# Layer 0's head norms on ScalarE with accumulated sums, two heads at a time, and layer 0's value scaling on VectorE

## The chip, the cores and the metric

The kernel runs on one core of one Trainium2 chip. The metric is the device time of one execution in microseconds; three executions of the kernel before gave 3661.22, 3663.64 and 3666.74 us, median 3663.64 us. The profile was taken of one more execution, with a span of 3660.5 us and a mean granted TensorE clock of 0.985.

## The reference

Two graph attention layers, one after the other, on 16 graphs of 1024 nodes with 256 features. Layer 0 (4 heads of 64 features), cut to what the change touches:

```
h = einsum('bnd,hde->bhne', x, W)                     # values per head
weight = leaky_relu(e_src[i] + e_dst[j]) masked by adj == 0
dst = softmax(weight) @ h + bias
out = relu(dst) + h
mu, var = out.mean(-1), out.var(-1)                   # over the 64 features of one head
out = (out - mu) / sqrt(var + 1e-6) * ln_gamma + ln_beta
x = layernorm(x + out)                                # over all 256 features
```

Layer 1 normalises its input, runs masked attention of 8 heads of 32 features in which queries, keys and values are the same tensor, adds the result, and applies an MLP of width 1024 with an exact Gelu; a last layer norm ends it.

## The kernel before

Everything in fp32 apart from the adjacency, which becomes a uint8 mask. A graph's 1024 nodes are 8 blocks of 128 rows, and 2 halves (n) of 512 rows.

Four engines execute an order fixed at build time (`manual_schedule`, L760). Two generators, `layer0()` and `layer1()`, yield after each step an estimated cost; the loop at L762 takes the next step from layer 0 of graph b+1 or from layer 1 of graph b. Which one is decided by `wanted()` and the table `COURSE` (L747): it says how far layer 0 should be when layer 1 is at a given place. So layer 0 of the next graph always runs beside layer 1 of this one, and in the steady state one graph after another repeats the same pattern. Post-processing is written as chains: `begin(chain, wait)` puts a generator on a list, and `advance` runs its next part when the planned clock has moved on by what the chain yielded. `complete(chain)` runs a chain's remaining parts at once. These yields decide only where instructions are recorded[...].

Layer 0 of a graph:

- `prepare` (L286): per pair of row blocks it transposes x (L227, copied by ScalarE at L230), turns the adjacency into a mask (transposes at L295, a squaring ScalarE activation with an accumulated sum at L296), and multiplies x by the weights W with the attention columns beside them (L322) into a PSUM tile `ph` named "acc". ScalarE then takes from `ph` the source terms (L323), `v0`'s last column exp(e) (L324), `dinv` (L325), and four times, once per head, the 64 value columns times that exp (L327): these products are the operand `v0` of the attention. VectorE adds the bias to the same `ph` for the residual `hb` (`take_h`, L347), at a planned distance of 1.5. "acc" has 2 buffers.
- `attention0` (L350): 16 steps. VectorE builds the weights `p` of a step (four instructions at L374, tile `p0`), TensorE multiplies them with `v0` (64 matmuls, L389). After each head of a half `relu_residual` (L418 to L430) divides, applies the relu and adds to `hb`.
- `after0` (L432): when the fourth head of a half is done, it normalises all 4 heads and 4 row blocks (128 x 1024 elements) together: sum (L445), centring (L446), square on ScalarE (L451), sum of squares (L454), variance (L455), `power` on GpSimd (L198) for the inverse root, gamma (L457), beta added to x (L458), scaling (L460), addition (L461). Then the layer norm over 256 features (L465 to L479) and layer 1's inputs: `normed` (L214 through `scale_shift`), x1 (L484), nT by transposes (L227, L233), v1 (L494).

Layer 1 of a graph: `attention1` (L502), 32 steps: TensorE makes four score tiles of 128x512 (L517) in the four PSUM buffers `ps`, ScalarE exponentiates them (L522), VectorE masks them one step later (L528), TensorE multiplies with the values two steps later (L535, L542). `mlp` (L629): first product (L637, also in `ps`), Gelu on ScalarE (L644), second product (L650), `last_norm` (L678).

`half(n)` (L724) hands layer 1 the results of `after0`; step jb = 4 of `attention1` is the first that needs half 1.

Of the kernel before, what the change touches and what calls it, by code (L numbers as in the profile page):

```python
# [31 lines left out]
F32 = mybir.dt.float32  # L32
# [3 lines left out]
AF = mybir.ActivationFunctionType  # L36
OP = mybir.AluOpType
PSUM = bass.MemoryType.PSUM

P = 128  # L40
# [10 lines left out]
def fast_path(  # L51
# [192 lines left out]
    def begin(chain, wait):  # L244
        chains.append([clock[0] + wait, chain])
# [40 lines left out]
    def prepare(b, hb, esr, v0, dinv, mask):  # L286

        def turn_mask(k):  # L290
            i = b * NB + k
            ak = adj_blocks.pop(i)
            pt = ps_a.tile([P, NB, P], BF16, name="acc")
            for j in range(NB):
                nc.tensor.transpose(pt[:, j, :], ak[:, j * P : (j + 1) * P], identb)  # L295
            nc.scalar.activation(  # L296
                mask[k // BPH][:, :, k % BPH * P : (k % BPH + 1) * P],
                pt,
                AF.Square,
                bias=shift_c,  # L300
                scale=-(NEAR0 + NEAR1),
                accum_out=types[:, i : i + 1],
            )
            load_adj(i + 3)

        for k in range(0, NB, GB):
            i = b * (NB // GB) + k // GB
            load_blocks(i + 1)
            xk = x_blocks.pop(i)
            xT = one.tile([P, DC, GB * P], F32, name="xT")  # L310
            transpose_rows(xT, xk)
            yield 0.45
            turn_mask(k)
            yield 0.5
            if k % BPH == 0:

                finish_norms(b - 1, k // BPH)
                hb.append(one.tile([P, BPH, D], F32, name=f"hb{k // BPH}"))
            for g in range(GB):
                ph = ps_a.tile([P, D + 2 * H0], F32, name="acc")  # L320
                for c in range(DC):
                    nc.tensor.matmul(ph, xT[:, c, g * P : (g + 1) * P], w0e[:, c, :], start=c == 0, stop=c == DC - 1)  # L322
                nc.scalar.copy(apart[g][:, :, 0], ph[:, D + H0 : D + 2 * H0])  # L323
                nc.scalar.activation(v0[:, k + g, :, HO], ph[:, D : D + H0], AF.Exp)  # L324
                nc.scalar.activation(dinv[:, k + g, :], ph[:, D : D + H0], AF.Exp, scale=-0.99)  # L325
                for hd in range(H0):
                    nc.scalar.mul(  # L327
                        v0[:, k + g, hd, 0:HO], ph[:, hd * HO : (hd + 1) * HO], v0[:, k + g, hd, HO : HO + 1]
                    )
                begin(take_h(hb[-1][:, (k + g) % BPH, :], ph), 1.5)  # L330
                yield 0.9
                if g == 0:
                    turn_mask(k + 1)
                    yield 0.5
            turning = turn_sources(esr[:, k * P : (k + GB) * P])
            begin(turning, 0.4)
        complete(turning)
# [5 lines left out]
        nc.scalar.copy(dst, es.rearrange("p g q -> p (g q)"))  # L343
        yield from ()

    def take_h(h, ph):
        nc.vector.tensor_add(h, ph[:, 0:D], bias0_r)  # L347
        yield from ()

    def attention0(b, hb, v0, esr, dinv, factors, mask, rinv):  # L350
# [81 lines left out]
    def after0(b, n, hd, av, o, rinv):  # L432


        relu_residual(av, hd, o, rinv)
        if hd < H0 - 1:
            return
        yield 1.5
        heads = [P, BPH * H0, HO]
        rowwise = [P, BPH, D]  # L440
        xl = one.tile(rowwise, F32, name="xl")
        load_x(xl, b, n * BPH, BPH)
        oh = o.rearrange("p g (h e) -> p (g h) e", e=HO)
        s = small.tile([P, BPH * H0], F32, name="s0")
# [6 lines left out]
        nc.scalar.activation(sq, o, AF.Square)  # L451
        yield 2.5
        v = small.tile([P, BPH * H0], F32, name="v0s")
        nc.vector.tensor_reduce(v, sq.rearrange("p g (h e) -> p (g h) e", e=HO), axis=mybir.AxisListType.X, op=OP.add)  # L454
        nc.vector.tensor_scalar(v, v, 1.0 / HO, EPS_HEAD, op0=OP.mult, op1=OP.add)  # L455
        r = power(v, BPH * H0, "r0")
        nc.vector.tensor_mul(o, o, lng0_r[:, None, :].to_broadcast(rowwise))  # L457
        nc.vector.tensor_add(xl, xl, lnb0_r[:, None, :].to_broadcast(rowwise))  # L458
        yield 3.0
        nc.vector.tensor_mul(oh, oh, r[:, :, None].to_broadcast(heads))  # L460
# [38 lines left out]
        handed[b, n] = x1, v1, nT  # L499
# [718 lines left out]
```

## Time and profile before

| engine | busy us | share of the span | instructions |
|---|---|---|---|
| PE (TensorE matmul) | 3452.5 | 94% | 64417 |
| PEld (weight load) | 2304.6 | 63% | 64417 |
| DVE (VectorE) | 2986.7 | 82% | 5328 |
| ACT (ScalarE) | 2156.0 | 59% | 4732 |
| POOL (GpSimd) | 384.5 | 11% | 360 |

Busy time is time in which an instruction of the engine was under way; a matmul that waits inside the pipeline still counts, so 94% is an upper bound of what TensorE did. DMA moved 33 GB/s on average and is not near a limit. Groups that the change touches, by line:

| line, engine | count | mean ns | busy us |
|---|---|---|---|
| L327 ACT, values times exp, 128x64 from PSUM | 512 | 315 | 118.6 |
| L451 ACT, square, 128x1024 | 32 | 1054 | 33.7 |
| L347 DVE, residual, 128x256 | 128 | 422 | 54.0 |
| L445, L454 DVE, sums | 32 each | 1215, 1214 | 38.9, 38.9 |
| L446, L457, L460 DVE, 128x1024 | 32 each | 1225, 1217, 1220 | 39.2, 39.0, 39.1 |
| L455 DVE, 128x16 | 32 | 174 | 5.6 |
| L198 POOL, 128x16 | 32 | 3815 | 122.1 |

Where the mean times the count exceeds the busy time, as at L327, neighbouring instructions overlapped: 118.6 us over 512 is 232 ns of engine time for each.

### The profile page before, as it was taken

How to read it: one execution, taken by the hardware profiler on the slowest of the kernel's cores; microseconds unless marked ns; L12 is line 12 of the kernel's file. 1: busy time of each engine (PE TensorE's matmuls, PEld its weight loads, DVE VectorE, ACT ScalarE, POOL GpSimd, SP SyncE). 2: the span in 40 equal slices, each digit the busy share in tenths (PEclk: the TensorE clock that was granted, in tenths of full speed). 3: DMA queues.
4: the chain of work that ended last, by engine and by line, in shares of the span. 5: the costliest groups of instructions: out<-in, count | busy, mean ns of one | idle time of the engine just before them, and what ended most of it. 6: DMA issues, size and time to landing. Idle time of an engine off the chain costs nothing.

```text
span 3660.5 us, 142025 instructions
## 1 busy us (share of the span) xinstructions
PE 3452.5 (94%) x64417; PEld 2304.6 (63%) x64417; DVE 2986.7 (82%) x5328; ACT 2156.0 (59%) x4732; POOL 384.5 (11%) x360
## 2 busy tenths in 40 slices
PE   5699999999999999999999999999999999999998
PEld 4458476575766757566585765757667575665846
DVE  4888788887878888788887988888788887888884
ACT  2474846647466574755747566474665747557464
POOL 0101101010110101101011010101101011010110
PEclk9799999999999999999999999999999999999999
DMA  4110201102010110201102011020101102010000
GB/s 106 28 23 16 46 6 42 18 26 36 13 41 12 33 29 14 45 7 38 23 16 46 6 40 20 26 36 13 41 12 32 31 14 45 7 38 9 16 6 14
DMA packets 77669, 97.67 MB, mean 27 GB/s; under 512 B 9088, under 2 KB 60160, under 8 KB 77056
## 3 DMA queue, kind: packets, MB, share of 16 engines
q0 software_dynamic: 18432, 33.56, 6.4%
q1 hardware_dynamic: 52736, 50.35, 4.4%
q8 instruction: 506, 8.29, 0.9%
q10 hardware_dynamic: 5888, 4.60, 0.4%
q14 instruction: 107, 0.88, 0.1%
HBM read 105.26 MB, written 16.78 MB: 33 GB/s over the span
## 4 chain that ended last, share of the span: by engine, by line
PE 63%; DVE 26%; issue 4%; ACT 3%; POOL 3%; DMA 1%; ACTq 0%; SPq 0%; DVEq 0%; POOLq 0%
PE ps L517 13%; PE po L535 10%; PE ps L637 9%; PE acc L389 9%; DVE p L528 7%; PE po L650 7%; PE po L542 6%; DVE p L374 6%; PE acc L322 3%; POOL r L198 3%; DVE st L203 2%; PE acc L295 1%; PE acc L227 1%; PE ps L363 1%; DVE mv L204 1%
## 5 line engine op out<-in xcount | busy, mean ns | idle before, releaser
L528 DVE TENSOR_TENSOR p<-p,mask 128x1024 f32<-128x1024 f32 x1024 | 1199.1, 1218 | 160.7 <-ACT p L522 156.9
L522 ACT ACTIVATE p<-ps 128x512 f32<-128x512 f32 x2048 | 1059.6, 614 | 329.6 <-PE ps L517 327.8
L517 PE MATMUL ps<-nT 32*128 32x512 f32 x4096 | 769.1, 654 | 12.6 <-ACT cb L365 10.0
L374 DVE SCALAR_TENSOR_TENSOR p<-cb,dinv,mask 128x512 f32<-128x512 f32 x1024 | 698.4, 744 | 0.5 <-ACT cb L365 0.5
L542 PEld LDWEIGHTS po<-v,p 128*32 128x32 f32 x32768 | 390.0, 110 | 334.2 <-issue 239.5
L389 PE MATMUL acc<-v,p 128*64 128x65 f32 x16384 | 556.4, 225 | 43.8 <-DVE p L374 42.7
L389 PEld LDWEIGHTS acc<-v,p 128*64 128x64 f32 x16384 | 511.5, 139 | 118.0 <-DVE p L374 65.2
L644 ACT ACTIVATE hid<-ps,b_sb 128x256 f32<-128x256 f32 x512 | 235.5, 471 | 555.4 <-PE ps L637 555.1
L535 PE MATMUL po<-p,v 128*32 128x512 f32 x2048 | 550.2, 612 | 10.4 <-DVE p L528 8.9
L535 PE MATMUL po<-p,unit 128*32 128x512 f32 x2048 | 549.5, 612 | 0.0
L637 PE MATMUL ps<-yT,w_sb 128*128 128x256 f32 x2048 | 491.6, 387 | 0.7 <-issue 0.7
L650 PE MATMUL po<-w_sb,hid 128*128 128x256 f32 x2048 | 465.0, 381 | 0.0
L650 PEld LDWEIGHTS po<-w_sb,hid 128*128 128x128 f32 x2048 | 385.4, 190 | 64.0 <-issue 11.4
L637 PEld LDWEIGHTS ps<-yT,w_sb 128*128 128x128 f32 x2048 | 376.2, 191 | 64.3 <-issue 12.2
L542 PE MATMUL po<-v,p 128*32 128x33 f32 x32768 | 387.6, 198 | 7.5 <-DVE o L584 3.1
L517 PEld LDWEIGHTS ps<-nT 32*128 32x128 f32 x4096 | 268.0, 186 | 170.8 <-issue 56.8
L535 PEld LDWEIGHTS po<-p,v 128*32 128x32 f32 x2048 | 78.7, 109 | 387.5 <-DVE p L528 204.5
L198 POOL TENSOR_TENSOR r<-v,mhalf 128x1 f32<-128x1 f32 (+1 forms) x160 | 158.1, 988 | 1009.2 <-DVE v L684 721.7
L296 ACT ACTIVATE mask<-acc,shift_c 128x1024 uint8<-128x1024 bf16 x128 | 144.3, 1127 | 44.3 <-PE acc L295 43.8
L322 PE MATMUL acc<-w0e,xT 128*128 128x264 f32 x512 | 146.2, 409 | 20.9 <-DVE hb L347 20.8
L278 POOL DMA_DIRECT2D ak<-in_adj_dram x128 | 69.7, 545 | 878.1 <-PE acc L295 864.7
L198 POOL TENSOR_TENSOR r<-v1s,mhalf 128x4 f32<-128x4 f32 x32 | 34.9, 1092 | 1132.2 <-DVE ranges L418 891.0
(116 smaller groups left out, 2929.2 us busy)
## 6 DMA issues: line engine op xcount, KB each, us to landing
ak<-in_adj_dram POOLq DMA_DIRECT2D x128, 256.0 KB, 3.9
xk<-in_x_dram SPq DMA_DIRECT2D x64, 256.0 KB, 2.8
xl<-in_x_dram SPq DMA_DIRECT2D x32, 512.0 KB, 4.0
out_dram<-z SPq DMA_DIRECT2D x128, 128.0 KB, 1.7
w_sb<-in_L_gnn_W_dram ACTq DMA_DIRECT2D x2, 1024.0 KB, 10.2
v<-in_L_gnn_a_src_dram ACTq DMA_DIRECT2D x1, 640.0 KB, 7.8
v<-in_L_gnn_a_dst_dram ACTq DMA_DIRECT2D x1, 640.0 KB, 3.8
w0e<-in_L_gnn_W_dram ACTq DMA_DIRECT2D x8, 32.0 KB, 7.3
```

The lines of the kernel that those rows point to most:

```text
L198: nc.gpsimd.tensor_tensor(r, src, mhalf[:, :n], op=OP.pow)
L322: nc.tensor.matmul(ph, xT[:, c, g * P : (g + 1) * P], w0e[:, c, :], start=c == 0, stop=c == DC - 1)
L374: nc.vector.scalar_tensor_tensor(p[:, i, :], cb[:, hd % PAIR, :], dinv[:, j2 + i, hd : hd + 1], mask[n][:, j2 + i, :], op0=OP.max, op1=OP. ...
L389: nc.tensor.matmul(av[at : at + TILE, q, :], ps[i // 2][:, i % 2, q * P + at : q * P + at + TILE], v0[:, j4 + i, hd, :], start=j4 + i == 0 ...
L517: nc.tensor.matmul(tiles[e], of_keys[q, quad, keys], of_queries[q, quad, :], start=True, stop=True)
L522: nc.scalar.activation(p[:, i, :], tiles[e + i], AF.Exp, scale=SCALE1)
L528: nc.vector.tensor_mul(p, p, mask[n][:, jb, None, :].to_broadcast([P, PAIR, HALF]))
L535: nc.tensor.matmul(moved[at * Q : (at + 1) * Q, :], v, ps[0][:, e, :], start=jb == 0, stop=jb == NB - 1)
L542: nc.tensor.matmul(held[at : at + Q, q, e, :], ps[1][:, e, q * P + at : q * P + at + Q], values[:, hd, :], start=jb == 0 and e == 0 and q ...
L637: nc.tensor.matmul(ph, w1_sb[:, c, f * P : (f + 1) * P], yT[:, c, q * P : (q + GB) * P], start=c == 0, stop=c == DC - 1,)
L644: nc.scalar.activation(hid[f // 4][:, f % 4, :], ph, AF.Gelu, bias=b1_sb[:, f : f + 1], scale=1.0)
L650: nc.tensor.matmul(po, hid[f // 4][:, f % 4, g * P : (g + 1) * P], w2_sb[:, f, :], start=f == 0, stop=f == FC - 1,)
```

## The change

The four scaling activations per row block in `prepare` leave ScalarE. VectorE does them as one product of 128x256 inside `take_h`, after the bias addition, with exp broadcast over the 64 columns of a head.

The norm per head runs for two heads of a half at a time, so a first chain starts when the second head is done and a second one after the fourth. VectorE sums (128x512 to 128x8) and scales by -1/64 to get minus the mean. ScalarE squares each 128x64 piece with minus the mean as its bias and accumulates the sum itself (8 activations per pair of heads, all into the same scratch tile `sq0`); centring and the second sum on VectorE go. After `power`, VectorE multiplies minus the mean by the inverse root, and ScalarE applies scale and shift with 8 Identity activations of 128x64, in place of VectorE's product. Gamma follows, on the two heads. Beta and x are added once for the half. The purpose is to even out the load of the two engines over the stages. The table `COURSE` is set to 1.42 and 15.0 where it had 1.45 and 14.0: layer 0 gets a little less of its work placed beside `attention1` and a little more beside `mlp`, and ends one planned unit earlier.

```diff
@@ prepare
-                for hd in range(H0):
-                    nc.scalar.mul(
-                        v0[:, k + g, hd, 0:HO], ph[:, hd * HO : (hd + 1) * HO], v0[:, k + g, hd, HO : HO + 1]
-                    )
-                begin(take_h(hb[-1][:, (k + g) % BPH, :], ph), 1.5)
+                begin(take_h(hb[-1][:, (k + g) % BPH, :], v0[:, k + g, :, :], ph), 1.5)
...
-    def take_h(h, ph):
+    def take_h(h, v, ph):
         nc.vector.tensor_add(h, ph[:, 0:D], bias0_r)
+        nc.vector.tensor_mul(
+            v[:, :, 0:HO],
+            ph[:, 0:D].rearrange("p (h e) -> p h e", e=HO),
+            v[:, :, HO : HO + 1].to_broadcast([P, H0, HO]),
+        )
@@ after0
         relu_residual(av, hd, o, rinv)
+        if hd % PAIR < PAIR - 1:
+            return
+        yield 1.0
+        heads = slice((hd - PAIR + 1) * HO, (hd + 1) * HO)
...
+        nc.vector.tensor_reduce(mean, oh, axis=mybir.AxisListType.X, op=OP.add)
+        nc.vector.tensor_scalar(mean, mean, -1.0 / HO, None, op0=OP.mult)
+        yield 1.5
...
+        for g, e in rows_of:
+            nc.scalar.activation(
+                sq, oh[:, g, e, :], AF.Square, bias=mean[:, g, e : e + 1], accum_out=v[:, g, e : e + 1]
+            )
+        yield 2.2
+        nc.vector.tensor_scalar(v, v, 1.0 / HO, EPS_HEAD, op0=OP.mult, op1=OP.add)
+        r = power(v.rearrange("p g e -> p (g e)"), BPH * PAIR, "r0").rearrange("p (g e) -> p g e", e=PAIR)
...
+        yield 2.5
+        nc.vector.tensor_mul(mean, mean, r)
+        if hd == H0 - 1:
+            nc.vector.tensor_add(xl, xl, lnb0_r[:, None, :].to_broadcast(rowwise))
+        yield 0.4
+        for g, e in rows_of:
+            nc.scalar.activation(
+                oh[:, g, e, :], oh[:, g, e, :], AF.Identity, bias=mean[:, g, e : e + 1], scale=r[:, g, e : e + 1]
+            )
+        yield 2.2
+        pair = o[:, :, heads]
+        nc.vector.tensor_mul(pair, pair, lng0_r[:, None, heads].to_broadcast([P, BPH, PAIR * HO]))
         if hd < H0 - 1:
             return
...
-        nc.vector.tensor_reduce(s, oh, axis=mybir.AxisListType.X, op=OP.add)
-        nc.vector.scalar_tensor_tensor(
-            oh, s[:, :, None].to_broadcast(heads), -1.0 / HO, oh, op0=OP.mult, op1=OP.add
-        )
-        yield 2.0
-        sq = one.tile(rowwise, F32, name="sq")
-        nc.scalar.activation(sq, o, AF.Square)
-        yield 2.5
...
-        nc.vector.tensor_reduce(v, sq.rearrange("p g (h e) -> p (g h) e", e=HO), axis=mybir.AxisListType.X, op=OP.add)
...
-        nc.vector.tensor_mul(oh, oh, r[:, :, None].to_broadcast(heads))
+        for first in range(PAIR - 1, H0 - 1, PAIR):
+            complete(norms[b, n, first])
         nc.vector.tensor_add(o, o, xl)
-        yield 2.0
+        yield 0.5
...
-    COURSE = [(0.0, 1.0), (ATTN1, 1.45), (WORK1 - 14.0, 2.0), (WORK1, 2.0)]
+    COURSE = [(0.0, 1.0), (ATTN1, 1.42), (WORK1 - 15.0, 2.0), (WORK1, 2.0)]
```

More of the change, by code (lines that the diff above doesn't have):

```diff
@@ L435, in after0 @@
         relu_residual(av, hd, o, rinv)
+        if hd % PAIR < PAIR - 1:
+            return
+        yield 1.0
+        heads = slice((hd - PAIR + 1) * HO, (hd + 1) * HO)
+        oh = o[:, :, heads].rearrange("p g (h e) -> p g h e", e=HO)
+        rows_of = [(g, e) for g in range(BPH) for e in range(PAIR)]
+        mean = small.tile([P, BPH, PAIR], F32, name="s0")
+        nc.vector.tensor_reduce(mean, oh, axis=mybir.AxisListType.X, op=OP.add)
+        nc.vector.tensor_scalar(mean, mean, -1.0 / HO, None, op0=OP.mult)
@@ new lines, in after0 @@
+        yield 1.5
+        v = small.tile([P, BPH, PAIR], F32, name="v0s")
+        sq = one.tile([P, HO], F32, name="sq0")
+        for g, e in rows_of:
[5 more added lines that the diff above has]
+        r = power(v.rearrange("p g e -> p (g e)"), BPH * PAIR, "r0").rearrange("p (g e) -> p g e", e=PAIR)
@@ new lines, in after0 @@
+        rowwise = [P, BPH, D]
+        if hd == H0 - 1:
+            xl = one.tile(rowwise, F32, name="xl")
+            load_x(xl, b, n * BPH, BPH)
+        yield 2.5
+        nc.vector.tensor_mul(mean, mean, r)
+        if hd == H0 - 1:
+            nc.vector.tensor_add(xl, xl, lnb0_r[:, None, :].to_broadcast(rowwise))
[4 more added lines that the diff above has]
+            )
@@ L436, in after0 @@
+        yield 2.2
+        pair = o[:, :, heads]
+        nc.vector.tensor_mul(pair, pair, lng0_r[:, None, heads].to_broadcast([P, BPH, PAIR * HO]))
         if hd < H0 - 1:
             return
[L438 to L444, printed above, removed]
-        nc.vector.tensor_reduce(s, oh, axis=mybir.AxisListType.X, op=OP.add)
@@ L446, in after0 @@
-        nc.vector.scalar_tensor_tensor(
-            oh, s[:, :, None].to_broadcast(heads), -1.0 / HO, oh, op0=OP.mult, op1=OP.add
-        )
-        yield 2.0
-        sq = one.tile(rowwise, F32, name="sq")
-        nc.scalar.activation(sq, o, AF.Square)
-        yield 2.5
-        v = small.tile([P, BPH * H0], F32, name="v0s")
-        nc.vector.tensor_reduce(v, sq.rearrange("p g (h e) -> p (g h) e", e=HO), axis=mybir.AxisListType.X, op=OP.add)
-        nc.vector.tensor_scalar(v, v, 1.0 / HO, EPS_HEAD, op0=OP.mult, op1=OP.add)
@@ L456, in after0 @@
[L456 to L460, printed above, removed]
+        for first in range(PAIR - 1, H0 - 1, PAIR):
+            complete(norms[b, n, first])
         nc.vector.tensor_add(o, o, xl)
-        yield 2.0
+        yield 0.5
         mv = small.tile([P, BPH, 2], F32, name="mv0")
```

## The prediction

> **What bounds the kernel.** I read the chain of waits first, then busy time by stage, then the timeline of one graph.
>
> ```profile
> PE 63%; DVE 26%; issue 4%; ACT 3%; POOL 3%; DMA 1%; ACTq 0%; SPq 0%; DVEq 0%; POOLq 0%
> ```
>
> TensorE carries most of the chain, VectorE a quarter; ScalarE's 3% says nothing yet, since a matmul that waits for a PSUM buffer counts as PE. So I cut one graph (222 us) into stages.
>
> ```profile
> 1492.36:1560.00 67.64, 63.31 (x1458) 33.73 (x1444) 49.26 (x69) 55.47 (x138) 3.96 (x9) 0.97 0.25 44
> 1560.00:1611.50 51.50, 50.13 (x1325) 27.34 (x1327) 50.14 (x64) 32.52 (x70) 1.46 (x2) 1.00 0.05 9
> 1611.50:1702.65 91.15, 89.10 (x1117) 75.92 (x1117) 74.96 (x174) 36.39 (x65) 15.11 (x11) 1.00 0.06 16
> 1702.65:1724.00 21.35, 18.62 (x288) 8.68 (x288) 20.85 (x44) 17.60 (x40) 4.12 (x4) 0.92 0.25 63
> ```
>
> Columns after the length: PE, PEld, DVE, ACT, POOL. Layer 1's attention beside `prepare` (first row) has ScalarE at 82%, VectorE at 73%. Its end, beside the first steps of `attention0`, has VectorE at 97%. The MLP (third row) has PE at 98%, ScalarE at 40%. The passage to the next graph has VectorE at 98%, ScalarE at 82%.
>
> PE's busy time hides its waits, so I compared runs of equal matmuls in the timeline: eight score matmuls (L517) follow one another in 1.07 us if nothing holds them.
>
> ```profile
> 1514.53 1.14 PE L517 MATMUL ps<-nT 32*128 32x512 f32 x8
> 1514.92 0.93 ACT L327 ACTIVATE v<-acc,v 128x64 f32<-128x64 f32 x4
> 1515.71 2.07 ACT L522 ACTIVATE p<-ps 128x512 f32<-128x512 f32 x4
> 1517.16 1.80 PE L517 MATMUL ps<-nT 32*128 32x512 f32 x8
> ```
>
> The four exponentials start only after L327's 0.93 us, the `ps` buffers come free late, and the next score run takes 0.66 us more. I summed such excess over the shortest of its kind for one graph (1702.65 to about 1925): some 23.6 us of 222. Of it 7.1 lie in the passage, 5.5 in the `prepare` stretch (3.65 in score runs like the one shown), 6.8 in the rest of `attention1`, 4.2 in the MLP. About 198 us per graph is TensorE's own work, which the change leaves alone. It can only move these 23.6.
>
> The passage hangs on the second half's norm:
>
> ```profile
> 1696.22 1.05 ACT sq L451
> 1697.30 1.23 DVE v0s L454
> ...
> 1698.81 3.83 POOL r L198
> 1702.65 1.24 DVE hb L460
> ...
> 1712.14 2.27 DVE p L528 x2
> ...
> 1716.86 2.08 ACT sq L214 x4
> ```
>
> Square, sum, power, scaling, then statistics between mask products (L528), then the activation whose result TensorE transposes for layer 1's fifth step: it waits 2.4 us there.
>
> [...]
>
> **The change, part by part.**
>
> *ScalarE, prepare.* L327 goes: 118.6 us, 0.93 us per row block, 7.4 per graph. Everything else on its queue there moves up by as much. In the 19 us of a pair of blocks TensorE's own work is about 17 us, and ScalarE then has about 15, so most score stalls of this stretch (0.66 to 0.81 each, below 0.93) should vanish: -3.5 us per graph, and -0.5 where mask transposes wait for the copy of x. The last two row blocks lie in the next stretch: -1.2.
>
> *VectorE, prepare.* 128 products of 128x256 from PSUM; L584 has the same form at 424 ns: +54.3 us, 3.4 per graph. This stretch has 18 us of VectorE idle, and the residual before it waited 73.1 us in all for L327, which ends. `ph` is held 0.42 us longer, but its buffer is wanted again some 4 us later: nothing.
>
> *VectorE, norms.* L446, L454, L460 go: -117.2 us. [...] Small ones at 0.16 to 0.17 (L455, L475): 64 times minus-mean and mean-times-root, and 32 more variances: +26. Net -81, or 5 us per graph, nearly all in the MLP and the passage. With the products VectorE falls by about 26, to 2961 us. In the MLP TensorE runs almost gapless, so this gives nothing directly there.
>
> *ScalarE, norms.* The trace has no 128x64 square with accumulation. [...] Its accumulator read is 209 ns at L296, where it overlaps the activation's end by 100. In the built order squares 2 to 8 of a burst each wait for the one before (same scratch tile). [...] I take 0.45, so 3.6 us per burst (2.7 to 4.3). [...] ScalarE rises by about 250, to 2404 us. The squares all fall into the MLP, which has 55 us of ScalarE idle per graph against 14.4 for them. Behind a burst wait Gelus (which free the `ps` buffers for L637) and exponentials for `cb`; on VectorE the variance waits for the burst, and `p` for TensorE queues behind it. Four buffers and the 2.02 us runs of L389 cover most: I charge +0.5 us per graph.
>
> *GpSimd.* Two 128x8 powers of 2.07 us replace one 128x16 of 3.8; the one on the passage's path is 1.7 us shorter.
>
> *The passage.* In the built order the last Identity burst stands behind the four exponentials of the next graph's first step, and gamma and the addition stand behind the mask products of the first two. From the first score run on (before: activation for TensorE at +14.2): exponentials end at +3.1, Identity +5.8, copy of x and second exponentials +8.4, masks +9.6, [...] statistics and variances +14.1, masks of the third step +16.4, residual and value product +17.3, then the activation at about +17.4. Before, scaling and addition were done ahead of those masks. So +3.2 us per graph on the path that ends the wait; the shorter power lies before it and is lost.
>
> *COURSE.* One `attention0` step (3 us of VectorE, 2 of TensorE) moves from the stretch where VectorE is at 97% to the MLP: -1.7 of the 6.8 us there; TensorE's work only moves.
>
> Sum per graph: -3.5 - 0.5 - 1.2 - 1.7 + 0.5 + 3.2 = -3.2 us. Fifteen graphs run so: -48. The first graph's layer 0 stands alone and bound by VectorE: about -3. 3663.6 - 51 = **3612 us**.
>
> **The rivals.** *The passage costs nothing*: the chain's later place is absorbed, since VectorE and ScalarE come to it with less backlog, and the bursts hide: -6.9 per graph, 15 x 6.9 + 3 = 107, **3557 us**. For it: the shorter power. Against: the built order, which puts Identity behind the exponentials. *ScalarE's bursts block the MLP*: half of each of four 3.6 us square bursts reaches TensorE through late Gelus and a waiting VectorE: 7.2 in place of 0.5, so +3.5 per graph, **3713 us**. For it: VectorE already waits 41.1 us for the one square (L451), and the MLP has no slack on TensorE. Against: 6 to 8 us of ScalarE idle at a time before Gelus. *A wash*: the passage takes 6 us, as masks slip a further step: -0.4, **3655 us**.
>
> **Chances.** Forecast 55%, free passage 20%, blocked MLP 15%, wash 10%. The range reaches most of the way to either side: 3540 to 3680, which also takes in the bounds of the square (0.9 us per burst either way, 4 bursts, 15 graphs: 50 us if all of it showed). Faster 76%, same 7%, slower 17%.
>
> **What would show it.** Score runs after L322 near 1.07 us in the `prepare` stretch (step 1); the wait of the transposes for the normed second half up from 2.4 to 5 to 6 us (passage); bursts of squares near 3.6 us, and L637 runs still at 1.73 to 1.83 (MLP); VectorE near 2960, ScalarE near 2400 us busy. I am wrong if the MLP lengthens by more than 3 us beyond the moved step, or if ScalarE's relief leaves the score runs as long as they are.

## The result, and the profile after

The changed kernel took **3750.99 us** (median of 4 runs, 3748.91 to 3751.62) against 3663.93 us before (4 runs): a ratio of 1.0237, 95% interval 1.0219 to 1.0254. It is 87 us slower, and 139 us above the forecast; the range ended at 3680.

First the page's line of busy times, then its chain of waits by engine.

```profile
PE 3509.3 (94%) x64417; PEld 2317.8 (62%) x64417; DVE 2942.9 (79%) x5584; ACT 2403.9 (64%) x5724; POOL 404.9 (11%) x392
```

```profile
PE 67%; DVE 18%; ACT 10%; issue 3%; POOL 1%; DMA 1%; ACTq 0%; SPq 0%; POOLq 0%; DVEq 0%
```

The work went where it was meant to go: VectorE 2943 us (forecast 2961), ScalarE 2404 (forecast 2404). For forms that the trace of before does not hold, the forecast used estimates of mine; in the changed kernel's trace a sum of 128x512 takes 680 ns and gamma on 128x512 688 ns, one square follows another after 0.47 us, and a burst of 8 Identity activations takes 2.76 us. TensorE runs the same 64,417 matmuls and is 57 us longer in doing so. In the chain VectorE falls from 26% to 18%, ScalarE rises from 3% to 10%. Evening out two busy times did not shorten the chain; it put ScalarE on it.

Busy time by stage of one graph (columns: length, then busy us and instructions of PE, PEld, DVE, ACT, POOL, then the granted TensorE clock). The cuts are at TensorE's own work: passage (first score run of a graph to the value matmuls after the transposes of `normed`'s second half), `prepare` stretch (to the last L322), late `attention1` (to the first product of the MLP), MLP. Of after:

```profile
1737.22:1762.56 25.34, 21.66 (x283) 10.04 (x284) 20.51 (x44) 19.31 (x44) 3.69 (x3) 0.80 0.20 53
1762.56:1827.31 64.75, 62.37 (x1474) 33.37 (x1476) 50.88 (x67) 49.97 (x112) 5.82 (x8) 1.00 0.26 44
1827.31:1870.64 43.33, 42.94 (x1159) 23.91 (x1160) 39.47 (x53) 25.66 (x53) 0.00 (x0) 1.00 0.01 3
1870.64:1965.50 94.86, 91.38 (x1120) 76.63 (x1124) 72.39 (x187) 55.43 (x150) 15.96 (x13) 1.00 0.05 16
```

Of before, cut in the same way, passage and MLP:

```profile
1702.65:1723.63 20.98, 18.25 (x281) 8.30 (x281) 20.48 (x44) 17.60 (x40) 4.12 (x4) 0.92 0.26 64
1836.20:1925.04 88.84, 86.93 (x1056) 73.95 (x1052) 74.01 (x171) 35.08 (x63) 15.10 (x11) 1.00 0.06 17
```

The two stages between took 59.86 and 52.71 us before (VectorE 49.93 in the latter, so 95%), at a clock of 1.00. The last three stages hold other numbers of matmuls than before, since COURSE moved work (the MLP 64 more, one step of `attention0`); their lengths can't be set side by side. So I use the measure of the prediction throughout: for each run of equal matmuls, the time from its start to the start of the next, less the shortest of its kind. That excess ("stall", us per graph, median of 13 graphs of the profiled execution) includes matmuls slowed by a lower clock (after four of the value matmuls L550 of the changed kernel the next four start 0.85 us later at half clock, 1747.40 to 1748.25, and 0.45 us later at full, 1753.10 to 1753.55), so stall and clock overlap. The last column is (1 - mean granted clock) x span of the whole execution, which is half of the time spent at half clock: in the traces of before and after the granted clock is 1.0 or 0.5 throughout. It is an upper estimate of what half clock took, since TensorE also waits in that time, and good to about 2 us.

| kernel | us | stall: passage | prepare | late | MLP | clock loss, whole run |
|---|---|---|---|---|---|---|
| before | 3663.9 | 8.0 | 6.7 | 6.3 | 5.3 | 55 |
| after | 3751.0 | 12.2 | 6.3 | 4.6 | 9.3 | 101 |

The sum goes up by 6.1 us per graph, some 92 us over 15 graphs, close to the 87 us. Two stages carry it: the passage +4.2 and the MLP +4.0.

### The profile page after: what moved, and what is told of

Read it like the earlier page. It is cut to its first block, busy times and chain, and to the rows that moved or that the text cites. A ratio compares the mean times of both kernels' runs of the same rounds, so it can differ in the third digit from the quotient of the medians.

```text
span 3748.8 us, 143287 instructions
## 1 busy us (share of the span) xinstructions
PE 3509.3 (94%) x64417; PEld 2317.8 (62%) x64417; DVE 2942.9 (79%) x5584; ACT 2403.9 (64%) x5724; POOL 404.9 (11%) x392
## 4 chain that ended last, share of the span: by engine, by line
PE 67%; DVE 18%; ACT 10%; issue 3%; POOL 1%; DMA 1%; ACTq 0%; SPq 0%; POOLq 0%; DVEq 0%
PE ps L532 16%; PE po L550 12%; PE acc L390 9%; PE po L665 8%; PE ps L652 7%; PE po L557 7%; DVE p L375 4%; DVE p L543 3%; ACT sq L450 3%; PE acc L322 3%; DVE st L203 2%; ACT hb L466 2%; ACT p L537 2%; PE acc L227 1%; PE ps L364 1%
## 5 line engine op out<-in xcount | busy, mean ns | idle before, releaser
L543 DVE TENSOR_TENSOR p<-p,mask 128x1024 f32<-128x1024 f32 x1024 | 1201.1, 1219 | 218.8 <-ACT p L537 217.2
L537 ACT ACTIVATE p<-ps 128x512 f32<-128x512 f32 x2048 | 1057.7, 607 | 379.6 <-PE ps L532 379.3
L532 PE MATMUL ps<-nT 32*128 32x512 f32 x4096 | 753.2, 666 | 31.3 <-ACT p L537 29.3
L375 DVE SCALAR_TENSOR_TENSOR p<-cb,dinv,mask 128x512 f32<-128x512 f32 x1024 | 697.3, 745 | 1.1 <-ACT cb L366 1.1
L390 PE MATMUL acc<-v,p 128*64 128x65 f32 x16384 | 577.7, 225 | 61.4 <-DVE p L375 58.8
L390 PEld LDWEIGHTS acc<-v,p 128*64 128x64 f32 x16384 | 517.6, 138 | 160.5 <-DVE p L375 72.9
L550 PE MATMUL po<-p,v 128*32 128x512 f32 x2048 | 566.6, 629 | 24.7 <-DVE p L543 24.7
L550 PE MATMUL po<-p,unit 128*32 128x512 f32 x2048 | 566.2, 629 | 0.0
L652 PEld LDWEIGHTS ps<-yT,w_sb 128*128 128x128 f32 x2048 | 375.2, 190 | 65.5 <-issue 11.4
L532 PEld LDWEIGHTS ps<-nT 32*128 32x128 f32 x4096 | 259.0, 188 | 173.6 <-ACT p L537 76.4
L550 PEld LDWEIGHTS po<-p,v 128*32 128x32 f32 x2048 | 79.1, 110 | 424.1 <-DVE p L543 215.5
L198 POOL TENSOR_TENSOR r<-v,mhalf 128x1 f32<-128x1 f32 (+1 forms) x160 | 172.4, 1077 | 836.3 <-DVE v L699 481.7
L450 ACT ACTIVATE sq<-hb,s 128x64 f32<-128x64 f32 x512 | 177.7, 347 | 90.9 <-DVE s L445 76.4
L366 ACT ACTIVATE cb<-ps 128x512 f32<-128x512 f32 x128 | 69.5, 595 | 177.5 <-PE ps L364 177.4
L466 ACT ACTIVATE hb<-hb,s,r 128x64 f32<-128x64 f32 x512 | 176.2, 436 | 1.0 <-DVE s L461 1.0
```

Of the source, the lines that this page charges most:

```text
L375: nc.vector.scalar_tensor_tensor(p[:, i, :], cb[:, hd % PAIR, :], dinv[:, j2 + i, hd : hd + 1], mask[n][:, j2 + i, :], op0=OP.max, op1=OP. ...
L390: nc.tensor.matmul(av[at : at + TILE, q, :], ps[i // 2][:, i % 2, q * P + at : q * P + at + TILE], v0[:, j4 + i, hd, :], start=j4 + i == 0 ...
L450: nc.scalar.activation(sq, oh[:, g, e, :], AF.Square, bias=mean[:, g, e : e + 1], accum_out=v[:, g, e : e + 1])
L466: nc.scalar.activation(oh[:, g, e, :], oh[:, g, e, :], AF.Identity, bias=mean[:, g, e : e + 1], scale=r[:, g, e : e + 1])
L532: nc.tensor.matmul(tiles[e], of_keys[q, quad, keys], of_queries[q, quad, :], start=True, stop=True)
L537: nc.scalar.activation(p[:, i, :], tiles[e + i], AF.Exp, scale=SCALE1)
```

## Experiments

Each ratio below is against runs of the kernel before on the same chip, whose medians were 3663.8 to 3667.3 us. In the changed kernel the score matmuls are L532, their exponentials L537, the mask products L543, the weights of `attention0` L375 and its value matmuls L390, the squares L450, Identity L466, residual and value product L343 and L344. An edit that adds or removes lines shifts these numbers.

### The change in three parts

*Value product alone on VectorE* (kernel before with the `prepare` and `take_h` parts of the change):

```diff
-                    nc.scalar.mul(
-                        v0[:, k + g, hd, 0:HO], ph[:, hd * HO : (hd + 1) * HO], v0[:, k + g, hd, HO : HO + 1]
-                    )
...
+        nc.vector.tensor_mul(
+            v[:, :, 0:HO],
...
```

> Only the value scaling moves to VectorE; norms and COURSE stay as before. Theory N (the norms on ScalarE cost the time, in the passage and the MLP; the value scaling helps a little, as the prepare stretch of the changed kernel lost 2.1 us of stall per graph): 2 us per graph x 15 = 30 us less than before, about 3634 us, ratio to before 0.992. Rival V (the value product on VectorE costs by itself, as VectorE is at 98% in the passage and the product comes on top): above 3690 us.

*The changed kernel with the value products back on ScalarE*, so that norms and COURSE remain:

> The changed kernel with the four scaling activations L327 back on ScalarE: norms by pairs on ScalarE and the new COURSE alone. Theory N: slower than the changed kernel by what the value scaling gave, 3751 + 30 = about 3780 us, ratio 1.032. Rival V: close to before, 3660 to 3690 us.

*COURSE alone* (kernel before):

```diff
-    COURSE = [(0.0, 1.0), (ATTN1, 1.45), (WORK1 - 14.0, 2.0), (WORK1, 2.0)]
+    COURSE = [(0.0, 1.0), (ATTN1, 1.42), (WORK1 - 15.0, 2.0), (WORK1, 2.0)]
```

> Before with the new COURSE (1.42, 15.0) alone. Theory D: the gain at the end of attention1 (1.7 us per graph) and the loss in the MLP nearly cancel, 3650 to 3675 us. Rival C (COURSE is a main part of the loss, since it leaves the MLP less slack): 3690 us or more.

| kernel | us | ratio | passage | prepare | late | MLP | clock loss |
|---|---|---|---|---|---|---|---|
| values alone | 3685.1 | 1.0052 [1.0035, 1.0069] | 8.0 | 6.4 | 7.1 | 6.5 | 81 |
| norms and COURSE | 3749.5 | 1.0232 [1.0215, 1.0249] | 12.1 | 6.3 | 4.0 | 9.3 | 94 |
| COURSE alone | 3694.4 | 1.0089 [1.0070, 1.0107] | 7.8 | 6.3 | 3.9 | 10.2 | 66 |

No part helps. Norms with COURSE make nearly the whole loss; COURSE alone costs 28 us, so norms cost 55 us on top of it. The table also tells the two stages apart: from COURSE alone to norms and COURSE the passage rises from 7.8 to 12.1, the MLP falls from 10.2 to 9.3. The passage's loss comes with the norms, the MLP's with COURSE. The value product, which should have brought the largest gain, costs 19 us by itself and 1.5 us, which is within the spread of the runs, in the changed kernel. Its `prepare` stalls fall by 0.3 us per graph, where the prediction had 4.0. For the first two parts, neither time that I had set down came.

### The passage: Identity between the exponentials

The chain of waits of the changed kernel, cut to the passage (start, us, what):

```profile
1738.26 2.04 ACT p L537 x4
1740.31 1.23 ACT hb L466 x4
1741.54 0.28 issue
1741.82 1.10 ACT hb L466 x3
...
1743.94 3.53 PE ps L532 x6
...
1755.73 1.96 ACT sq L214 x4
```

The last Identity burst (L466) is on the chain: it stands between the exponentials of the first and second step, so the second step's begin 5.0 us after the first's (1738.24 to 1743.28 in ScalarE's timeline), the score tiles stay taken, and TensorE, after 1.90 us without work, takes 3.53 us for its third score run where it takes 1.97 in the next kernel:

```profile
1743.94 3.53 PE L532 MATMUL ps<-nT 32*128 32x512 f32 x8 [1.90 <-ACT p L537]
```

From 1744.96 on, part of this run is at half clock as well (the granted clock is 0.50 from there to 1751.79). The activation for TensorE (L214, `sq`, at 1755.60 in ScalarE's timeline) begins 18.5 us after the first score run (at 1737.09), against 14.2 before. The test records the chain of the last pair of half 1 sooner:

```diff
+        last = hd == H0 - 1 and n == NH - 1
-        yield 1.0
+        yield 0.2 if last else 1.0
...
-        yield 1.5
+        yield 0.2 if last else 1.5
...
-        yield 2.2
+        yield 1.0 if last else 2.2
```

The three later distances go from 2.5, 0.4 and 2.2 to 1.0, 0.2 and 0.8 in the same way.

> The changed kernel with shorter planned distances in the chain of the second half's last pair alone (0.2, 0.2, 1.0, 1.0, 0.2, 0.8), so that the last Identity burst stands ahead of the next graph's first exponentials on ScalarE, and gamma and the addition ahead of its first mask products on VectorE, as scaling and addition stood before. Theory P (the passage costs 4 to 4.5 us per graph because of that order): 15 x 4.2 = 63 us less than the changed kernel, about 3688 us, and the activation of the normed half back at about 14 us after the first score run (18.4 in the changed kernel). Rival M (the loss is in the MLP, and the passage's wait is only where it shows): within 10 us of 3751.

It took 3679.7 us (1.0043 [1.0026, 1.0060]): 71 us less than the changed kernel, with the passage at 7.1 in place of 12.2 and clock loss down to 40 us. In ScalarE's timeline no Identity stands there any more, and the second exponentials begin 2.4 us after the first:

```profile
1708.64 2.06 ACT L538 ACTIVATE p<-ps 128x512 f32<-128x512 f32 x4
...
1711.03 2.13 ACT L538 ACTIVATE p<-ps 128x512 f32<-128x512 f32 x4
...
1721.28 2.08 ACT L214 ACTIVATE sq<-hb,t,r 128x256 f32<-128x256 f32 x4 [0.67 <-DVE t L208]
```

The first score run of that graph began at 1707.33, so L214 is at +14.0, about where it was before the change. As a control the kernel *before* got its half-1 chain sooner in the same way (its distances 1.5, 2.0, 2.5, 3.0 and 2.0 become 0.4, 0.4, 0.8, 1.5 and 0.5 for half 1):

> Before with shorter planned distances in the chain of the second half alone (0.4, 0.4, 0.8, 1.5, 0.5 for 1.5, 2.0, 2.5, 3.0, 2.0), no arithmetic moved. Theory P (the passage hangs on where that chain stands in the engines' order): its square, power and scaling come some 2 us earlier, the passage's stall falls by about 2 us per graph, 3634 us. Rival: what it waits for is mask products and exponentials whatever the chain's place, 3660 to 3668 us.

3663.3 us, 0.9993 [0.9982, 1.0004], passage 8.3: no change. So the 71 us are not a slack that any earlier chain would have found; they undo what the chain's place had cost. The edit moves the whole chain, VectorE's gamma and addition with it; Identity's share alone was not taken apart.

### Half clock: filling the waits with useless work

The passage's clock is 0.80 in the table of stages, against 0.92: half clock took about 5.1 of its 25.3 us, 1.7 of 21.0 before. That came with the waits, but did it come of them? The next kernel is the changed one with nothing moved; two waits are filled with transposes whose results are overwritten: `fill` is 12 for the first transposes of half 1 into nT.

```diff
+        for i in range(fill):
+            nc.tensor.transpose(pt[:, i % DC, i // DC % GB, :], ident, ident)
...
-            for j in range(NB):
+            for j in range(NB * (3 if k == 0 else 1)):
```

> The changed kernel (3751.0 us, half clock costs 4.9 us per graph) with useless transposes that fill TensorE's two waits in the passage: 12 of the identity into the tile of nT ahead of those of normed's second half, and the mask transposes of a graph's first row block three times over. Nothing else moves. Theory A (half clock follows a stretch in which TensorE was poorly filled): the half clock at about +8 us after the passage's first score run shrinks from 6.8 us to 3.4 or none, clock loss falls to 1 to 3 us per graph, 3700 to 3730. Theory B (half clock does not hang on these waits): clock loss stays near 4.9, 3750 to 3775, with the transposes' own time on top.

It took **3723.6 us** (1.0165 [1.0149, 1.0182]), 27 us less than the changed kernel, with more work on TensorE. Its passage:

```profile
1729.50:1753.98 24.48, 23.12 (x320) 12.16 (x323) 19.46 (x43) 19.25 (x45) 3.69 (x3) 0.86 0.21 55
```

PE busy is 94% of the stage where it was 85%, and the clock 0.86. Over the whole run clock loss falls from 101 to 48 us. So in this kernel half clock hung on how well the stretch was filled. In the graph shown, TensorE's longest gaps ahead of the two spells are 1.90 and 1.54 us; no longer wait stood there. The filling is worth 27 us although it takes time itself. That these are a part of the 71 us of the earlier chain is likely, since that chain's clock loss is 40 us too, but the two were not run together.

### Square bursts in the MLP

Squares 2 to 8 of a burst write the scratch tile that the one before wrote. Giving each its own slot takes that wait away:

```diff
-        sq = one.tile([P, HO], F32, name="sq0")
+        sq = one.tile([P, BPH * PAIR, HO], BF16, name="sq0")
...
-                sq, oh[:, g, e, :], AF.Square, bias=mean[:, g, e : e + 1], accum_out=v[:, g, e : e + 1]
+                sq[:, g * PAIR + e, :], oh[:, g, e, :], AF.Square, bias=mean[:, g, e : e + 1], accum_out=v[:, g, e : e + 1]
```

> The changed kernel with a scratch slot of its own (bf16) for each of the 8 squares of a burst, so that none waits for the one before. Theory B (the MLP loses 3.7 us per graph because VectorE and Gelu wait for bursts of 3.75 us): the pitch falls from 0.47 to about 0.35 us, a burst to 2.8 us, the MLP's stall by 1 to 1.5 us per graph, 3728 to 3736 us. Rival Q (the bursts' place in the queue counts, not their length): 3745 to 3752 us.

3720.0 us (1.0142 [1.0125, 1.0159]), 31 us less. ScalarE's timeline of one burst, changed kernel first:

```profile
1662.04 0.33 ACT L450 ACTIVATE sq<-hb,s 128x64 f32<-128x64 f32 x1
1662.28 0.19 ACT L450 ACTIVATION_READ_ACCUMULATOR sq<-hb,s 128x1 f32 x1
1662.49 0.35 ACT L450 ACTIVATE sq<-hb,s 128x64 f32<-128x64 f32 x1
```

```profile
1650.06 0.33 ACT L450 ACTIVATE sq<-hb,s 128x64 bf16<-128x64 f32 x1
1650.30 0.19 ACT L450 ACTIVATION_READ_ACCUMULATOR sq<-hb,s 128x1 f32 x1
1650.40 0.33 ACT L450 ACTIVATE sq<-hb,s 128x64 bf16<-128x64 f32 x1
```

From square to square it is 0.47 us (1662.49 to 1662.97 in the trace), and 0.33 with own slots: the accumulator read hides, the wait for the scratch tile did not. The slots are also bf16 where the tile was fp32. One square takes 0.33 us with either (the first of each burst above); no run has fp32 slots, so a share of the type in the shorter distance is not excluded. A burst falls from 3.74 us (1662.04 to 1665.78) to 2.75 (1650.06 to 1652.81): 1 us by 4 bursts by 15 graphs is 60 us, of which 31 reached the end (I had expected 15 to 23). VectorE waits behind it, in the list of waits of the changed kernel and of this one:

```profile
DVE v0s L454 <- ACT sq L450: 107.4, 45, 3.7
```

```profile
DVE v0s L454 <- ACT sq L450: 60.8, 30, 2.7
```

MLP stalls fall from 9.3 to 7.8, the passage's from 12.2 to 11.4. Both repairs together, the edits of the two kernels in one:

> e4 (Identity ahead of the next graph's first exponentials) and e5 (a scratch slot for each square) together. If the passage and the squares' bursts are two separate losses, they add: 71 + 31 us off the changed kernel, about 3650 us, ratio to before 0.996. If the squares' gain came through the passage alone, nothing is added: about 3675 us.

**3650.3 us** (0.9957 [0.9941, 0.9974]): the 71 and the 31 add up (101 measured), and the kernel is 0.4% faster than before. Passage 7.3, `prepare` 6.3, late 4.4, MLP 7.8.

### COURSE: which step meets which queue

Against the kernel before, the repaired one still loses 2.5 us per graph in the MLP, and COURSE alone lost 4.9 there. VectorE's timeline at the MLP's start in the changed kernel, then TensorE's:

```profile
1875.41 1.23 DVE L619 TENSOR_TENSOR o<-o,x 128x1024 f32<-128x1024 f32 x1
1876.66 0.43 DVE L203 BATCH_NORM_STATS2 st<-o 128x6 f32<-128x256 f32 x1
...
1879.01 2.73 DVE L375 SCALAR_TENSOR_TENSOR p<-cb,dinv,mask 128x512 f32<-128x512 f32 x4
```

```profile
1879.89 2.58 PE L390 MATMUL acc<-v,p 128*64 128x65 f32 x64 [1.29 <-DVE p L375]
```

The step of `attention0` that COURSE moved into the MLP is recorded after layer 1's norm, so its weights `p` stand behind the residual and four statistics on VectorE, and TensorE waits. Two tries with the repaired kernel, the old COURSE and one step further:

```diff
-    COURSE = [(0.0, 1.0), (ATTN1, 1.42), (WORK1 - 15.0, 2.0), (WORK1, 2.0)]
+    COURSE = [(0.0, 1.0), (ATTN1, 1.45), (WORK1 - 14.0, 2.0), (WORK1, 2.0)]
...
+    COURSE = [(0.0, 1.0), (ATTN1, 1.40), (WORK1 - 15.0, 2.0), (WORK1, 2.0)]
```

> e6 with COURSE set back to 1.45 and 14.0. Theory D (the new COURSE puts attention0 steps of the MLP behind layer 1's own norm on VectorE, some 2.5 us of stall at the MLP's start, and gains 1.7 in the stretch before it): within 15 us of e6, 0.8 us per graph to the better side, about 3640 us. Rival: the old COURSE brings VectorE's full stretch back and loses 1.7 us per graph, 3675 us.

> The kernel with the earlier chain and a scratch slot per square (3650.3 us), with COURSE at 1.40 in place of 1.42: one step more of layer 0 moves from attention1 to the MLP. Theory A (an attention0 step put into the MLP's start stalls it behind layer 1's norm on VectorE): MLP 9 us or more, late attention1 4 or less, time 3655 to 3680. Theory B (the MLP has room for it): MLP stays near 7.8, 3640 or less.

1.45/14.0 gave 3695.0 us (1.0086 [1.0069, 1.0103]), slower than either theory had it: the MLP falls to 5.7, but late `attention1` rises to 10.7. 1.40/15.0 gave **3620.7 us** (0.9875 [0.9858, 0.9891]): MLP 5.5, late 3.7. The loss I had expected from a further step did not come. In the graph looked at, one step has its `p` ahead of the norm, which begins after 1814.38, and the next has it behind but comes late enough on TensorE:

```profile
1809.39 2.73 DVE L375 SCALAR_TENSOR_TENSOR p<-cb,dinv,mask 128x512 f32<-128x512 f32 x4
...
1818.69 2.73 DVE L375 SCALAR_TENSOR_TENSOR p<-cb,dinv,mask 128x512 f32<-128x512 f32 x4
```

There TensorE runs 16 matmuls of the first product from 1818.02, and its value run of that step starts at 1821.67 without a wait, at 2.09 us. COURSE is no dial from less to more: 1.45, 1.42 and 1.40 are three meetings of steps with queues. The kernel before at 1.40:

> The kernel before with COURSE 1.40 and 15. Theory A (the placement alone brings what the repaired kernel gained, 30 us): 3630 to 3645. Theory B (only norms on ScalarE leave VectorE free enough in the MLP for one step more): as COURSE 1.42 in the kernel before or slower, 3690 to 3710, MLP stalls of 9 us or more per graph.

3656.2 us (0.9978 [0.9971, 0.9986]), MLP 7.8: neither of the values I had set down. Placement alone brings 8 us, and most of the repaired kernel's gain at 1.40 needs the norms on ScalarE.

### The value product, on either engine

Products back on ScalarE, with the repaired norms, at each COURSE (1.45, 1.42, 1.40):

```diff
-                begin(take_h(hb[-1][:, (k + g) % BPH, :], v0[:, k + g, :, :], ph), 1.5)
+                for hd in range(H0):
+                    nc.scalar.mul(
+                        v0[:, k + g, hd, 0:HO], ph[:, hd * HO : (hd + 1) * HO], v0[:, k + g, hd, HO : HO + 1]
+                    )
+                begin(take_h(hb[-1][:, (k + g) % BPH, :], ph), 1.5)
```

> Norms on ScalarE by pairs with the earlier chain and a scratch slot per square, value products on ScalarE, COURSE as before (1.45, 14.0). The same with the value product on VectorE took 3695.0 us, with 10.7 us of stalls per graph in the late part of attention1 and 5.7 in the MLP. Theory A: those late stalls come from the value product of VectorE in the stretch that VectorE bounds, and from the half clock after them, as the value product alone with the old COURSE lost 19 us: late falls to about 6.5, half clock under 2 us per graph, 3620 to 3640. Theory B: the pair norms themselves overload VectorE there under the old COURSE: late stays at 9 or more, about 3690.

> The kernel with the earlier chain and a scratch slot per square (3650.3 us), with the four value products per row block back on ScalarE. Theory A: with the changed COURSE the value product is worth nothing on either engine, as with the changed kernel (3749.5 against 3751.0): within 8 us of 3650, late attention1 stalls near 4.0 us per graph, prepare 6.3. Theory B: VectorE is the tighter engine and the product costs it 3.4 us per graph, part of it on the path: 3635 or less. Theory C (the prediction's step): ScalarE's value products delay the exponentials: 3690 or more, prepare above 8.

> As the kernel with the earlier chain, a scratch slot per square and COURSE 1.40 (3620.7 us), with the four value products per row block back on ScalarE. Theory A (the value product is worth nothing on either engine): 3615 to 3627. Theory B (the product on VectorE costs where VectorE bounds, as the old COURSE showed with 39 us): 3612 or less. Theory C (it relieves ScalarE in prepare, as predicted): 3630 or more.

| COURSE | norms as before, products ScalarE | norms repaired, products ScalarE | norms repaired, products VectorE |
|---|---|---|---|
| 1.45/14 | 3663.9 | 3655.7, 0.9974 [0.9963, 0.9985] | 3695.0 |
| 1.42/15 | 3694.4 | 3655.4, 0.9970 [0.9959, 0.9982] | 3650.3 |
| 1.40/15 | 3656.2 | **3604.5, 0.9839 [0.9822, 0.9855]** | 3620.7 |

The last row's middle is the fastest kernel of all. The norms on ScalarE are worth 8, 39 and 52 us down the columns, once their bursts are placed well; the product on VectorE costs 39 us, gains 5 (little more than the spread of the runs), costs 16. At the old COURSE with the products on ScalarE I had expected 3620 to 3640 or 3690 us, and 3655.7 is neither; the other two came as one of their theories had it. At the old COURSE it is the late stretch: stalls 6.3 with the products on ScalarE, 10.7 with them on VectorE. TensorE's line at its edge in the latter:

```profile
1792.22 1.16 PE L322 MATMUL acc<-w0e,xT 128*128 128x264 f32 x4 [1.92 <-DVE v L344]
```

The projection of the last row block waits for the PSUM buffer that the product now releases, with layer 1's statistics ahead on VectorE. With the products on ScalarE this wait is 1.12 us, for the residual. Half clock follows at 1793.3: the value matmuls after the next score run take 1.06 us each, where those before the wait took 0.59 to 0.62, and the granted clock is 0.91 in the late stretch, against 1.00 with the products on ScalarE. Is that wait the cause? Two kernels begin residual and product sooner, ahead of the statistics: the value product alone, and the repaired kernel at the old COURSE.

```diff
-                begin(take_h(hb[-1][:, (k + g) % BPH, :], v0[:, k + g, :, :], ph), 1.5)
+                begin(take_h(hb[-1][:, (k + g) % BPH, :], v0[:, k + g, :, :], ph), 0.5)
```

> Value product on VectorE alone, COURSE and norms as before (3685.1 us), with the residual and the product begun 0.5 after a row block's projection in place of 1.5, so that they stand ahead of layer 1's statistics on VectorE. Theory A (TensorE's wait at L322 for the PSUM buffer that the product releases, and the half clock after it, make the 19 us): L322's wait falls from 31 us in all to under 8, half clock at the end of prepare vanishes, 3655 to 3668. Theory B (VectorE's 3.4 us per graph in the stretch that it bounds): 3680 or more.

> The repaired kernel with COURSE as before (3695.0 us; late attention1 stalls 10.7 us per graph, half clock 4.7) with the same change of 1.5 to 0.5. Theory A: late falls to 6.5 or less, clock loss to about 1.7, 3645 to 3660, as with the products on ScalarE (3655.7). Theory B: 3685 or more.

The waits for the product at L322, first with the value product alone, then with it begun sooner:

```profile
PE acc L322 <- DVE v L344: 31.0, 19, 1.9
```

```profile
PE acc L322 <- DVE v L344: 2.2, 4, 0.6
```

The wait went, and clock loss fell in the whole run, from 81 to 66 us with the value product alone and from 93 to 82 in the repaired kernel, but the times hardly moved: 3681.9 us (1.0043 [1.0026, 1.0060], 3 us less, within the spread of its runs) and 3683.9 us (1.0042 [1.0028, 1.0056], 11 us less). The `prepare` stalls, of which that wait is a part, fell by some 2 us per graph in both, to 4.3; late rose from 7.1 to 8.8 in the one, and fell only from 10.7 to 9.4 in the other. The list of waits shows where the time went. TensorE's wait for the mask products, with the value product alone and then with it begun sooner:

```profile
PE po L536 <- DVE p L529: 6.8, 14, 1.7
```

```profile
PE po L536 <- DVE p L529: 52.8, 33, 2.4
```

In the repaired kernel it rose from 4.3 to 52.3 us. The theory that the one wait makes the loss fell: removed, it came back as a wait for the next thing that VectorE makes. That points to VectorE's queue at that place rather than to one buffer: each product takes 413 ns of VectorE near a stretch where VectorE was at 95% before the change. That fits, but no run isolates it. How the 16 us at 1.40 arise is open, and so is why the MLP's stalls rise from 5.3 to 6.5 with the value product alone.

### The score runs that the prediction meant to shorten

After the change there is no value product ahead of the exponentials, and the score run still takes 1.77 us:

```profile
1795.93 1.14 PE L532 MATMUL ps<-nT 32*128 32x512 f32 x8
1797.09 2.06 ACT L537 ACTIVATE p<-ps 128x512 f32<-128x512 f32 x4 [0.75 <-PE ps L532]
1798.56 1.77 PE L532 MATMUL ps<-nT 32*128 32x512 f32 x8
```

ScalarE was idle for 0.75 us before the exponentials. They begin when the four score tiles end, together, and take 2.06 us. From the start of the score run to the end of its exponentials that is 3.22 us (1795.93 to 1799.15). TensorE's next score run comes 2.63 us after the last one began, finds tiles taken, and is 0.63 us longer than the 1.14 of an unhindered one; 3.22 - 2.63 = 0.59 is about that. I call it the loop of four tiles. Two lines with no value product ahead of the exponentials show it too, the first from late `attention1` of the kernel before, the second from `prepare` with the value product alone on VectorE:

```profile
1817.97 1.77 PE L517 MATMUL ps<-nT 32*128 32x512 f32 x8
```

```profile
1749.25 1.77 PE L518 MATMUL ps<-nT 32*128 32x512 f32 x8
```

That second kernel has the order of the kernel before in all else, so its score runs can be set against those of before, place by place (start to next start, median over the graphs). The six long ones of `prepare` go from 1.73 (twice) and 1.88 (twice) to 1.70, and from 1.29 and 1.57 to 1.11. That is a gain of 1.06 us per graph. TensorE's wait at the last L322 takes 0.79 of it back, as the last mask transposes show: from their start to that of L322 it is 2.54 us in place of 1.75. The test of the loop itself, on the kernel before, shortens only the exponentials:

```diff
-                    nc.scalar.activation(p[:, i, :], tiles[e + i], AF.Exp, scale=SCALE1)
+                    nc.scalar.activation(p[:, i, 0:384], tiles[e + i][:, 0:384], AF.Exp, scale=SCALE1)
```

> The kernel before with layer 1's exponentials on 384 of 512 columns; the other 128 columns of p are filled with the mask by VectorE, so a quarter of layer 1's exponentials is left out. Theory A (the score runs of 1.70 us are the loop of four score tiles ending together and four exponentials of 2.06 us, whether or not a value product lies there): the exponentials take about 1.64 us and the lone score runs of the prepare stretch fall from 1.70 to about 1.3. Theory B (the prediction's: they wait for ScalarE's value products ahead of the exponentials): they stay near 1.7 where a value product lies ahead.

The exponentials take 1.65 us. The score runs of 1.73 us fall to 1.31, those of 1.88 to 1.46, though a value product (0.93 us) lies ahead of each as before; the lone one in late `attention1` without a value product falls from 1.70 to 1.27. `prepare` stalls fall from 6.7 to 4.8; one run, with a quarter of the exponentials left out, took 3609.3 us against 3664.8. So the loop sets most of the length, and L327, which runs while the score tiles are being made, adds 0.03 us to a run, and 0.18 to 0.46 where the mask's activation lies ahead too.

## Why the prediction was wrong

Its terms per graph against the stalls measured, in us: `prepare` -4.0, measured -0.4; late -1.2 - 1.7 = -2.9, measured -1.7; MLP +0.5, measured +4.0; passage +3.2, measured +4.2. The misses, 3.6 + 1.2 + 3.5 + 1.0 = 9.3, by 15 graphs are the 139 us. Both signs of being wrong came: the MLP of the graph shown is 6.0 us longer, 4.0 beyond the moved step's 2.0, and score runs of 1.70 us remain.

- **"ScalarE, prepare: most score stalls of this stretch should vanish": failed.** L327 stood ahead of exponentials wherever a run of this stretch was long, and I took the neighbour for the cause. The lines in the prediction speak against it: the score tiles are complete at 1514.53 + 1.14 = 1515.67, and the exponentials begin at 1515.71, so L327's 0.93 us held them up by 0.04. Moving L327 alone shortened the score runs by 1.06 us per graph, not 3.5, and the wait at L322 took most of that back. The narrow exponentials show the loop of four tiles. A count of ScalarE's work against TensorE's in 19 us could not show that, since the bound is the order within one step.
- **"VectorE, prepare: its buffer is wanted again some 4 us later: nothing": failed at the old COURSE**, where L322 waits for the product 1.92 us (1.12 for the residual without it); right at 1.42, where that wait totals 2.2 us in the whole run.
- **"TensorE's work only moves" (COURSE): failed.** The late stretch did gain, 2.4 us with COURSE alone; the moved step met layer 1's norm on VectorE, 4.9 were lost in the MLP, and the whole cost 28 us. I priced where it left and not what it would be queued behind where it came to.
- **"I charge +0.5 us per graph" (square bursts): mis-sized.** The square at 0.45 was an estimate of mine that no trace of before showed; it came out right (0.47), the burst too (3.74 us for 3.6). Own slots alone brought 31/15 = 2.1 us per graph, so at least that much of the bursts had reached TensorE (1.5 of it in the MLP by the stalls), not 0.5. The rival of blocked bursts named these waits, but put 7.2 us of them on the MLP, where 4.0 were measured and COURSE alone makes 4.9. With the norms on top the MLP stalls less than with COURSE alone (9.3 for 10.2), bursts and all. VectorE's lighter load, which the prediction put at nothing there, is the likely reason; that is argued and not shown.
- **"So +3.2 us per graph on the path that ends the wait": the order right, the wait wrong, the size short.** Identity stands where the built order put it; L214 came at +18.5 for a forecast of +17.4. But the wait of the transposes fell, from 2.4 to 1.6 us, where I expected 5 to 6: TensorE was held earlier, at the score runs behind Identity, and then ran at half clock.
- **Missing altogether: the clock.** By the column above up to 46 of the 87 us are half clock. In the changed kernel the passage of nearly every graph has two spells of it, of 6.83 and 3.41 us, where before most had one of 3.41. The prediction has no term for it, though its own stage table showed 0.92 in the passage. A term for waits that leaves out the clock is too small where half clock follows them, as here.

## What to carry to other kernels

Before taking work off an engine because it stands ahead of a wait, find a place where the same wait occurs without it; here a run of 1.70 us without L327 was in the trace all along. Price moved work by the queue it arrives in, and bursts on a shared engine by their place in its order: the same norms cost 55 us or brought up to 52, by where the chain and one `attention0` step stood and whether the squares shared a tile. When two parts of a change go together, measure each alone and repaired, for the worst loss hid the good part, and the part forecast as best was the one to leave out.

## What the runs showed of the hardware that I had not expected

Kernels whose TensorE is busy for some 94% of the span still spend 80 to 200 us of some 3600 to 3750 at half clock (twice the clock loss of 40 to 101 us), and in the steady graphs of before and after the longest wait of TensorE ahead of a spell, or at its start, was 1.5 to 2.3 us; a spell lasted 3.41 or 6.83 us. Adding useless transposes in two waits made the changed kernel 27 us faster (3751.0 to 3723.6) and its mean granted clock rise from 0.973 to 0.987. And an accumulating square of 128x64 costs ScalarE 0.33 us, its accumulator read of 0.19 us being hidden, if each has its own output slot (bf16 here); with one shared scratch tile it is 0.47 us.
